# Two attention layers on one core: three tiles instead of two for the values' output, three instead of four for the loads of v, and statistics placed later

## The chip, the cores and the metric

The kernel runs on one core of a Trainium2 chip, as one launch. The metric is device time in microseconds (us). The kernel before takes 3063.1 us, the median of three runs (3060.73, 3063.10 and 3066.85).

## What is computed

The input x is 4 images of 256 channels and 64 by 64 pixels, in float32. Two layers follow each other, each of the form x + layer(gn(x)), where gn is a group norm over 32 groups of 8 channels. Cut to what matters:

```
# layer 0, 8 heads of 32 channels: keys and values come from 2x2 patches, so 1024 of them per image
q = conv1x1(gn(x)); k = conv2x2_stride2(gn(x)); v = conv2x2_stride2(gn(x))
x = x + softmax(scale * q.(k + pos)) . v
# layer 1: each image is cut into 4 areas of 1024 pixels, which attend to themselves
q, k, v = conv1x1(gn(x))
out = softmax(scale * q.k) . v
x = x + conv1x1(out + depthwise_conv7x7(v))
```

Both group norms need the mean and the variance of a whole image before the first of its pixels can be normalized.

## The kernel before, in words

**Blocks, units, steps, phases.** The eight blocks of work are layer 0 for images 0 to 3 (A0 to A3), then layer 1 for images 0 to 3 (B0 to B3). A block is 16 units: 8 chunks of 512 pixels times 2 groups of 4 heads. A unit has 8 steps, one for each 128 keys. The main loop (L1159) takes one and a half steps at a time and calls that a phase, so that three steps are two phases. In a phase TensorE computes the scores of the next step and a half (`s`, L428), then does a piece of side work if one is due (a projection, a slice of the convolution, a row of softmax divisors), then multiplies the exponentials of the phase before with v (`av`, L494). ScalarE makes the exponentials (`p`, L469 and L480); VectorE adds them up to the softmax divisors (`acc`, L504). The scores fill three pairs of PSUM banks in turn, the exponentials six tiles of SBUF (`PB`).

**What sets the order.** Everything beside scores, exponentials and sums is planned ahead by unit and step: `at(unit, step, f)` puts `f` into the main loop at that step, and `task_at` hands a job to a list from which the main loop takes pieces. The order of the instructions on each engine is therefore written by the planner and kept; engines meet through semaphores. All loads and stores but those of the softmax divisors stand in one queue, that of SyncE (SP). An instruction whose wait is not yet over holds up all that stands behind it on its engine or queue. Tiles of one tag share a fixed number of buffers (`bufs`); a tile that takes a used buffer waits for the last reader of what lay there.

**What the change touches.**
- `plan_a` (L551) prepares and runs layer 0 for one image. Ahead of the image's own block it loads each of the 8 chunks of x once for statistics (`look`, L560, tile `xs`), and some steps later, the `lag` of L627, `add_stats` (L563) runs two `bn_stats` on the chunk, one for each half of the channels. `plan_norm` (L335, called at L629) joins the statistics to a shift and a scale. The tiles `xs` share the 6 buffers of the tag `chunk` (L104) with the other chunk tiles: `xa` and `hq` (x to be normalized for keys and values, and for queries), `xc` (residual), `hv` (below), `xm` and `cv` (layer 1).
- `plan_values` (L948) makes v of layer 1 for one chunk: it loads the chunk of layer 0's result (`hv`, L955), ScalarE normalizes it (L957, through L392), TensorE projects it, ScalarE writes the projection to a tile `vout` whose margins VectorE has zeroed (L963, L964, L975), and SP stores `vout` in two layouts: `vala`, for attention (L980), and `vals`, for the convolution (L988). `vout` has 2 buffers.
- `plan_b` (L705) runs layer 1 for one image. For each area it reads v back from `vala` in four loads (`load_v`, L740, tile `vc`, 4 buffers), and VectorE transposes each (`make_v`, L744, L749) into the tile that `av` reads.

Both `vout` and `vc` take 2304 bytes of each partition and buffer.

Of the kernel before, what the change touches and what calls it, by code (L numbers as in the profile page):

```python
# [9 lines left out]
FP = mybir.dt.float32  # L10
# [5 lines left out]
P = 128  # L16
# [11 lines left out]
RC = CH // WW  # L28
# [7 lines left out]
TY, TX, NY, XT, NP, TC = 16, 2, 4, WW // 2 + 4, 88, 8  # L36
# [24 lines left out]
def direct_path(  # L61
# [22 lines left out]
    pool = ctx.enter_context(tc.tile_pool(name="work", bufs=1))  # L84
# [93 lines left out]
    def ps_side(name):  # L178
        if now[0] < 0:
            return ps_pair(name)[:, 0, :]  # L180
        return psum.tile([P, CH], FP, tag=banks[1], name=name, bufs=1)
# [4 lines left out]
    def at(g, j, f):  # L186
        g, j = g + int(j // NKT), int(j % NKT)
        plan.setdefault((g, j), []).append(f)
# [127 lines left out]
    def soon(f):  # L316

        if now[0] < 0:
            f()
        else:  # L320
            quick.append(f)
# [13 lines left out]
    def plan_norm(key, g, j):  # L335

        name = f"{key[0]}{key[1]}"
        made = {}

        def aggregate():  # L340
            for tag, cols in (("mv", 2), ("gmean", 1), ("dev", 1), ("gvar", 1)):
                shape = [P, CT, cols] if cols > 1 else [P, CT]
                made[tag] = pool.tile(shape, FP, tag=tag, name=f"{tag}_{name}", bufs=2)
            mv = made["mv"]
            for t in range(CT):
                V.bn_aggr(out=mv[:, t, :], in_=stats[key][:, t].rearrange("p c s -> p (c s)"))

        def means():
            mv, mean, dev = made["mv"], made["gmean"], made["dev"]
            ps = ps_side(f"gm_{name}")[:, :CT]  # L350
            T.matmul(ps, lhsT=gmat, rhs=mv[:, :, 0], start=True, stop=True)
            S.copy(mean, ps)
            V.tensor_sub(dev, mv[:, :, 0], mean)
            V.tensor_mul(dev, dev, dev)
            V.tensor_add(dev, dev, mv[:, :, 1])

        def variances():
            ps = ps_side(f"gv_{name}")[:, :CT]
            T.matmul(ps, lhsT=gmat, rhs=made["dev"], start=True, stop=True)
            S.activation(made["gvar"], ps, AF.Identity, bias=eps)  # L360
            norm = pool.tile([P, 2, CT], FP, tag="norm", name=f"norm_{name}", bufs=8)
            shift, rstd = norm[:, 0, :], norm[:, 1, :]
            G.tensor_tensor(rstd, made["gvar"], neghalf, ALU.pow)
            if key == ("A", 0):
                V.scalar_tensor_tensor(shift, made["gmean"], -1.0, rstd, ALU.mult, ALU.mult)
            else:
                G.tensor_tensor(shift, made["gmean"], rstd, ALU.mult)
                G.tensor_scalar(shift, shift, -1.0, None, ALU.mult)
            norms[key] = shift, rstd
            known[key] = phase[0] if now[0] >= 0 else -4  # L370

        def quietly(f, n):
            f()
            if key == ("A", 0):
                keep_busy(n)

        if key == ("A", 0):
            at(g - 1, 0, lambda: keep_busy(44))
        at(g, j, aggregate)
        at(g, j + (2 if g >= 0 else 1), lambda: soon(lambda: quietly(means, 4)))  # L380
        at(g, j + (6 if g >= 0 else 3), lambda: soon(lambda: quietly(variances, 10)))
# [169 lines left out]
    def plan_a(b, u, prep):  # L551

        key = ("A", b)

        early = prep - (5 if b == 1 else 8 if b else 0)
# [68 lines left out]
        for c in range(NCH):  # L624
            at(early + c // 2, 4 * (c % 2), lambda c=c: look(c))
            for t in range(CT):
                lag = (5 + 2 * t if b == 1 else 8 + 2 * t if b else 3)  # L627
                at(early + c // 2, 4 * (c % 2) + lag, lambda c=c, t=t: add_stats(c, t))
        plan_norm(key, early + (5 if b > 1 else 4), 3 if b > 1 else 4 if b else 1)  # L629
        for a in range(NAREA):  # L630
            g = prep + (1 + 3.6 * a if b == 1 else 0.05 + 3.7 * a if b else 6 + 2.2 * a)
            at(0, int(NKT * (g - 2.4)), lambda a=a: load(a))
# [48 lines left out]
        for c in range(NCH):  # L681
            g = u + 2 * c
# [22 lines left out]
    def plan_b(b, u):  # L705
        key = ("B", b)
# [11 lines left out]
        kvs, vcs = {}, {}  # L718
# [19 lines left out]
                ks["B", b, a] = k  # L738

        def load_v(a, n):  # L740
            vcs[a, n] = pool.tile([P, 2, 4 * TX, XT], FP, tag="vc", name=f"vc_{b}_{a}_{n}", bufs=4)
            nc.sync.dma_start(vcs[a, n], vala[b][a][:, :, 2 * n : 2 * n + 2].rearrange("t c h f x -> (t c) h f x"))

        def make_v(a, n):  # L744

            if n == 0:
                kvs["v"] = v_tile(("B", b, a))
            v, vc = kvs["v"], vcs.pop((a, n))
            V.transpose(  # L749
                out=v[:, :, 2 * n * HD : 2 * (n + 1) * HD].rearrange("p j (h x) -> p h j x", h=2),  # L750
                in_=vc[:, :, :, 1 : 1 + WW // TX],
            )
            if n == 3:
                vs["B", b, a] = v
# [18 lines left out]
        for a in range(NAREA):  # L773
            g = u + 4 * a
            at(g - 6, 3, lambda a=a: load(a))
            for t in range(CT):
                at(g - 5, 2 + 3 * t, lambda a=a, t=t: later(("hs", b, a), lambda: norm(a, t), after(key, since[a] + 6), True))
            for n in range(4):
                task_at(
                    NKT * (g - 4) + 1 + 4 * n, 2, make_k, a, n // 2, n % 2, due=g - 0.4, ready=normed("hs", b, a)  # L780
                )
            for n in range(4):
                at(g - 4, 3 + 2 * n, lambda a=a, n=n: load_v(a, n))
                at(g - 2, 1 + 2 * n, lambda a=a, n=n: make_v(a, n))
        for c in range(NCH):
            for qd in range(2):
                task_at(
# [76 lines left out]
        for c in range(NCH):  # L864
            g, j = (u + 2 * c + 4, 1) if b < B - 1 or c < NCH - 2 else (u + 2 * c + 3, 7)
# [82 lines left out]
    def plan_values(b, c, start):  # L948

        made = {}  # L950

        def load():
            made["at"] = phase[0]
            made["h"] = chunk_tile(f"hv_{b}_{c}")
            nc.sync.dma_start(made["h"], xmid[b][c])  # L955

        def norm(t):  # L957
            normalize(("B", b), made["h"][:, t, :], made["h"][:, t, :], t)

        def values(t):  # L960
            vout = pool.tile([P, RC, TX, XT], FP, tag="vout", name=f"vout_{b}_{c}_{t}", bufs=2)
            written.append(phase[0])
            V.memset(vout[:, :, :, 0], 0.0)  # L963
            V.memset(vout[:, :, :, 1 + WW // TX :], 0.0)  # L964
            settle(("hv", b, c))
            h = made["h"]
            ps = ps_side(f"vals_ps_{b}_{c}_{t}")
            for tt in range(CT):
                product(
                    ps, lhsT=wqkv_sb[:, tt, 2, t * P : (t + 1) * P], rhs=h[:, tt, :],  # L970
                    start=(tt == 0), stop=(tt == CT - 1),
                )
                if tt == 0:
                    yield
            S.activation(  # L975
                vout[:, :, :, 1 : 1 + WW // TX], ps.rearrange("p (r x f) -> p r f x", r=RC, f=TX), AF.Identity,
                bias=bqkv_sb[:, 2, t : t + 1],
            )
            for n in range(2):
                nc.sync.dma_start(  # L980
                    vala[b][c // 2][2 * (c % 2) + n, :, 4 * t : 4 * t + 4].rearrange("c h f x -> h c (f x)"),
                    vout[:, 4 * n : 4 * n + 4].rearrange("p r f x -> p (r f x)"),
                )

            out = vout.rearrange("p r f x -> p r (f x)")
            for f in range(TX):
                at_row = (1 - f) * (XT - 1)
                nc.sync.dma_start(  # L988
                    vals[b][HALO + c * RC : HALO + (c + 1) * RC, f, t * P : (t + 1) * P, :].rearrange("r p x -> p r x"),
                    out[:, :, at_row : at_row + XT],  # L990
                )
            if t == CT - 1:
                stored[b, c] = True

        when = int(start * NKT)
        at(0, when - 5, load)
        for t in range(CT):
            at(0, when + 5 + t, lambda t=t: later(("hv", b, c), lambda: norm(t), after(("B", b), made["at"] + 6), True))
        for t in range(CT):
            task_at(  # L1000
                when + 7, 2, values, t, due=start + 4,
                ready=lambda: written[-2] + 4 <= phase[0] and normed("hv", b, c)(), lag=1 + 4 * t,
            )
# [153 lines left out]
    f = step = 0  # L1157
    before, credit = [], 0.0
    while f < PHASES or before or plan or side or quick or norms_left or to_add or to_divide:  # L1159
# [16 lines left out]
        _, rate = pressure()  # L1176
# [10 lines left out]
        elif due and not begun():  # L1187
            done_den = 1
            copies[0] += 1
            g = to_divide.popleft()  # L1190
# [644 lines left out]
```

## Time and profile before

| what | value |
|---|---|
| the profiled execution, its own time | 3063.53 us |
| its span, from the first to the last instruction | 3061.5 us |
| median of the three timed runs | 3063.1 us |
| granted clock of TensorE over the span | 0.998 |
| TensorE (PE) busy | 3032.8 us, 99% |
| VectorE (DVE) busy | 2526.2 us, 83% |
| ScalarE (ACT) busy | 2455.9 us, 80% |
| GpSimd (POOL) busy | 433.8 us, 14% |
| share of TensorE in the chain that ended last | 91% |

A page of the profile shows one execution. Busy time counts instructions of an engine, without those that issue DMAs. The timeline lists start and duration, the engine, the line of the kernel, the operation, and out<-in by tile names without their numbers; instructions of one kind that stand together are merged (x3). What stands in brackets is how long the engine stood idle just before, and what ended that. In rows of SP's queue (SPq) the duration is that of issuing, not of moving the data. The chain that ended last follows the last instruction back, at each step to what released it.

### The profile page before, as it was taken

Reading aid. Unit: us, or ns where it says so; the run is one execution under the profiler, and the core shown is the slowest. Engines: PE = TensorE matmul, PEld = TensorE weight load, DVE = VectorE, ACT = ScalarE, POOL = GpSimd, SP = SyncE. Lnnn points to the kernel's source line nnn. Section 1 sums busy time; section 2 is a strip of 40 time slices with the busy share of each in tenths; the row PEclk is TensorE's granted clock in tenths of the full one; section 3 lists DMA queues with packets and bytes.
Section 4 is the critical chain, followed back from the end, with each engine's and each line's share of the span. In section 5 each row is a group of like instructions: output and inputs, shape, how many; then the busy total and the mean of one; then the engine's idle time right before and its main releaser. Section 6 shows DMA issues by size and latency. Waiting matters only on the chain.

```text
span 3061.5 us, 108320 instructions
## 1 busy us (share of the span) xinstructions
PE 3032.8 (99%) x47254; PEld 1280.0 (42%) x47254; DVE 2526.2 (83%) x2769; ACT 2455.9 (80%) x2988; POOL 433.8 (14%) x794
## 2 busy tenths in 40 slices
PE   9999999999999999999999999999999999999998
PEld 6444434444344444333444444444434444443332
DVE  3788988889887787878888888788878888888888
ACT  3888888888887888888888877788777787878885
POOL 0011111111111111111111111111111111111111
PEclk9999999999999999999999999999999999999999
DMA  5244533466354557777866677667755565553232
GB/s 191 51 101 98 126 92 73 109 142 165 83 140 133 143 152 175 189 161 194 204 175 162 156 176 185 152 171 178 176 127 145 144 159 143 149 139 79 50 71 62
DMA packets 644250, 422.73 MB, mean 138 GB/s; under 512 B 409740, under 2 KB 552572, under 8 KB 643768
## 3 DMA queue, kind: packets, MB, share of 16 engines
q1 hardware_dynamic: 619384, 380.11, 49.3%
q0 software_dynamic: 24384, 35.62, 5.1%
q8 instruction: 373, 6.11, 0.9%
q14 instruction: 109, 0.89, 0.1%
HBM read 317.28 MB, written 97.05 MB: 135 GB/s over the span
## 4 chain that ended last, share of the span: by engine, by line
PE 91%; DMA 3%; DVE 2%; ACT 2%; issue 2%; SPq 1%; POOL 0%; DVEq 0%; ACTq 0%; POOLq 0%
PE s L428 31%; PE av L494 26%; PE k0ps L167 4%; PE den L513 4%; PE v0ps L167 4%; PE q1ps L167 4%; PE k1ps L167 4%; PE conv_ps L1048 4%; PE q0ps L167 4%; PE ops L167 4%; PE vals_ps L167 3%; DVE acc L504 1%; ACT p L469 1%; DMA vals<-vout 1%; DMA rows<-vals 1%
## 5 line engine op out<-in xcount | busy, mean ns | idle before, releaser
L504 DVE TENSOR_TENSOR acc<-acc,p 128x1024 f32<-128x1024 f32 x1790 | 2117.4, 1220 | 382.7 <-PE av L494 285.7
L469 ACT ACTIVATE p<-s 128x1024 f32<-128x1024 f32 x1194 | 1159.8, 1025 | 419.3 <-PE s L428 407.6
L480 ACT ACTIVATE p<-s 128x1024 f32<-128x1024 f32 x598 | 619.8, 1036 | 1.5 <-DVE acc L504 0.7
L428 PE MATMUL s<-q,k_A 32*64 32x256 f32 (+1 forms) x10928 | 541.1, 494 | 4.1 <-ACT p L469 3.5
L428 PE MATMUL s<-q,k_B 32*64 32x512 f32 (+1 forms) x10912 | 537.1, 494 | 2.8 <-ACT p L469 2.4
L494 PE MATMUL av<-p,v_A 128*32 128x256 f32 (+1 forms) x4784 | 451.4, 486 | 0.0
L494 PE MATMUL av<-p,v_B 128*32 128x512 f32 (+1 forms) x4776 | 449.4, 487 | 0.0
L428 PEld LDWEIGHTS s<-q,k_B 32*64 32x64 f32 x10912 | 266.0, 130 | 325.1 <-PE s L428 60.4
L428 PEld LDWEIGHTS s<-q,k_A 32*64 32x64 f32 x10928 | 263.2, 130 | 329.1 <-PE s L428 58.5
L537 POOL DMA_DIRECT2D rb<-recs x508 | 251.4, 501 | 510.3 <-DMA recs<-few 497.9
L535 POOL DMA_DIRECT2D recs<-few x127 | 71.3, 561 | 1719.9 <-DVE sums L534 1600.3
L494 PEld LDWEIGHTS av<-p,v_B 128*32 128x32 f32 x4776 | 149.2, 110 | 264.5 <-issue 238.3
L494 PEld LDWEIGHTS av<-p,v_A 128*32 128x32 f32 x4784 | 149.5, 110 | 227.5 <-issue 186.0
L469 ACT ACTIVATE acc<-s 128x1024 f32<-128x1024 f32 x172 | 167.0, 1023 | 80.6 <-PE s L428 80.2
L513 PE MATMUL den<-acc,ones 128*32 128x512 f32 x1024 | 138.5, 605 | 0.9 <-DVE xm L831 0.9
L167 PE MATMUL ops<-cv,wp_sb 128*32 128x512 f32 x1024 | 126.6, 605 | 4.7 <-DVE xm L831 3.5
L527 POOL DMA_DIRECT2D few<-den_sb x127 | 90.5, 713 | 271.9 <-ACT den_sb L526 271.3
L167 PE MATMUL vals_ps<-hv,wqkv_sb 128*32 128x512 f32 x1024 | 124.9, 598 | 0.5 <-issue 0.5
L167 PE MATMUL q1ps<-h,wqkv_sb 128*32 128x512 f32 x1024 | 124.9, 599 | 0.0
L167 PE MATMUL k1ps<-h,wqkv_sb 128*32 128x512 f32 x1024 | 123.0, 597 | 1.7 <-ACT cout L1059 0.9
L167 PE MATMUL q0ps<-hq,wq_sb 128*32 128x512 f32 x1024 | 124.0, 597 | 0.1
L167 PE MATMUL k0ps<-taps,wkv 128*32 128x256 f32 x2048 | 123.9, 383 | 0.0
(102 smaller groups left out, 2089.5 us busy)
## 6 DMA issues: line engine op xcount, KB each, us to landing
rows<-vals SPq DMA_DIRECT2D x384, 195.9 KB
rb<-recs POOLq DMA_DIRECT2D x508, 64.0 KB, 3.6
share<-vals SPq DMA_DIRECT2D x128, 195.9 KB
vala<-vout SPq DMA_DIRECT2D x128, 144.0 KB
vals<-vout SPq DMA_DIRECT2D x128, 144.0 KB
vc<-vala SPq DMA_DIRECT2D x64, 288.0 KB
band<-mats SPq DMA_DIRECT2D x96, 176.0 KB
hq<-in_x SPq DMA_DIRECT2D x32, 512.0 KB
```

Source lines behind the costliest of these rows:

```text
L167: T.matmul(out[cols, :], lhsT=lhsT[:, cols], rhs=rhs, start=start, stop=stop)
L428: T.matmul(out[n : n + WIDE], lhsT=unit[2]()[rows, unit[0], j * P + n : j * P + n + WIDE], rhs=unit[1]()[rows, cols], start=True, stop=True,)
L469: S.activation(p, (a, b)[n], AF.Exp, scale=SCALE)
L480: S.activation(p, c.rearrange("p b (l n) -> p b l n", l=2), AF.Exp, scale=SCALE)
L494: T.matmul(out, lhsT=v[:, j, unit[0] * P + HD * h : unit[0] * P + HD * h + HD], rhs=rhs, start=(j == 0 and not u), stop=(j == NKT - 1), sk ...
L504: V.tensor_add(to, to, p)
L513: T.matmul(dens[g][HD * h : HD * h + HD, :], lhsT=ones, rhs=p(h), start=(n == 0), stop=(n == len(sets) - 1),)
L527: G.dma_start(few[:, 0, :], den_sb[0:P:HD, :].rearrange("h (q n) -> h q n", n=CH // HD))
L535: G.dma_start(recs.rearrange("h (q n) -> (h q) n", n=CH // HD), few[:, 1, :])
L537: G.dma_start(rb[HD * h : HD * h + HD, :], recs[h : h + 1, :].to_broadcast([HD, CH]))
L1048: T.matmul(ps[HD * m : HD * m + HD, (2 * k + i) * size : (2 * k + i + 1) * size].rearrange("p (y x) -> p y x", y=NY), lhsT=band[:, half].r ...
```

## The change

Four edits, in three places:

```
--- before
+++ after
@@ plan_a
         for c in range(NCH):
             at(early + c // 2, 4 * (c % 2), lambda c=c: look(c))
             for t in range(CT):
-                lag = (5 + 2 * t if b == 1 else 8 + 2 * t if b else 3)
+                lag = (5 + 2 * t if b == 1 else 11 + 2 * t if b else 3)
                 at(early + c // 2, 4 * (c % 2) + lag, lambda c=c, t=t: add_stats(c, t))
-        plan_norm(key, early + (5 if b > 1 else 4), 3 if b > 1 else 4 if b else 1)
+        plan_norm(key, early + (5 if b > 1 else 4), 4 if b > 1 else 4 if b else 1)
@@ plan_b
         def load_v(a, n):
-            vcs[a, n] = pool.tile([P, 2, 4 * TX, XT], FP, tag="vc", name=f"vc_{b}_{a}_{n}", bufs=4)
+            vcs[a, n] = pool.tile([P, 2, 4 * TX, XT], FP, tag="vc", name=f"vc_{b}_{a}_{n}", bufs=3)
             nc.sync.dma_start(vcs[a, n], vala[b][a][:, :, 2 * n : 2 * n + 2].rearrange("t c h f x -> (t c) h f x"))
@@ plan_b, g is the unit at which area a begins
             for n in range(4):
-                at(g - 4, 3 + 2 * n, lambda a=a, n=n: load_v(a, n))
-                at(g - 2, 1 + 2 * n, lambda a=a, n=n: make_v(a, n))
+                at(g - 4, 7 + 2 * n + 5 * (n == 3), lambda a=a, n=n: load_v(a, n))
+                at(g - 2, 0 + 2 * n + 3 * (n == 3), lambda a=a, n=n: make_v(a, n))
@@ plan_values
         def values(t):
-            vout = pool.tile([P, RC, TX, XT], FP, tag="vout", name=f"vout_{b}_{c}_{t}", bufs=2)
+            vout = pool.tile([P, RC, TX, XT], FP, tag="vout", name=f"vout_{b}_{c}_{t}", bufs=3)
```

The output tile of the values gets a third buffer and the loads of v lose one, so that the memory stays the same. For images 2 and 3 the two `bn_stats` of a chunk stand three steps, two phases, further behind the chunk's load, and the joining of the statistics one step later. The loads of v for an area stand four steps later (the fourth nine steps later), and their transposes one step earlier (the fourth two steps later). No instruction is added or removed.

## The prediction

> **What bounds the kernel now.** I read the page's shares first, then the chain that ended last.
>
> ```profile
> PE 3032.8 (99%) x47254; PEld 1280.0 (42%) x47254; DVE 2526.2 (83%) x2769; ACT 2455.9 (80%) x2988; POOL 433.8 (14%) x794
> ...
> PE 91%; DMA 3%; DVE 2%; ACT 2%; issue 2%; SPq 1%; POOL 0%; DVEq 0%; ACTq 0%; POOLq 0%
> ```
>
> TensorE is busy for 3032.8 of 3061.5 us, so all its idle time is 28.7 us. The change adds and removes no instruction, and the built programs have the same order on TensorE, ScalarE and GpSimd; only places on VectorE and in SP's queue differ. A gain can only come out of those few microseconds, and a loss only through a new wait that reaches TensorE.
>
> So I looked for phases that last too long. From the starts of the score rows in the timeline, phases with equal work last equally long: 4.62 us with a full projection, 4.65 with a slice of the convolution, 3.76 with the divisors (the shortest of each kind). What a phase takes above that is a stall that TensorE felt. For whole-run waits on the values' output I took the view of the tile `vout`:
>
> ```profile
> its engine sat idle before it (us, times) until:
>   DMA vals<-vout: 10.3, 4
> ```
>
> Writers of `vout` waited 10.3 us for its stores, four times, on ScalarE and VectorE together. The timeline around the worst place:
>
> ```profile
> 1383.23 0.81 ACT L392 ACTIVATE hq<-hq,norm_A 128x512 f32<-128x512 f32 x1 [2.04 <-DMA hq<-in_x]
> ...
> 1385.92 2.00 PE L428 MATMUL s<-q,k_A 32*64 32x256 f32 x32 [1.17 <-ACT p L469]
> ...
> 1388.28 0.70 ACT L975 ACTIVATE vout<-vals_ps,bqkv_sb 128x512 f32<-128x512 f32 x1 [1.50 <-DMA vals<-vout]
> 1388.33 0.07 DVE L963 MEMSET vout<- 128x16 f32 x1 [4.70 <-DMA vals<-vout]
> ...
> 1389.03 1.11 PE L1048 MATMUL conv_ps<-rows,band 88*32 88x128 f32 x32 [1.11 <-ACT vout L975]
> 1389.67 1.03 ACT L469 ACTIVATE p<-s 128x1024 f32<-128x1024 f32 x1 [0.69 <-DVE acc L504]
> ```
>
> Two things are to be seen. The store of `vout` holds ScalarE and VectorE, and TensorE feels it through the bank of `conv_ps` and through late sums. And the first two rows give a rate that I use below: when a load (`hq`) kept ScalarE idle for 2.04 us, TensorE idled for 1.17, so about 0.87 us of a wait on ScalarE is covered.
>
> **The third buffer of vout.** What TensorE lost beside these waits: the phase from 1240.81 to 1246.86 took 6.05 instead of 4.65 (1.40); 1385.92 to 1392.24, 6.32 instead of 4.65 (1.67); the next two, with late sums, 5.23 instead of 4.62 (0.61) and 4.57 instead of 3.76 (0.81). Together **4.49 us**. With three buffers the writer at 1388.28 needs the stores that the zeroing at 1368.45 waited for, long over; the one at 1242.90 needs stores issued by 1214.1. So the waits go. The hq wait at 1383.23 (a phase of 5.00 instead of 3.76) stays: it is another tile. Ends: 4.49 if all goes, 1.40 + 1.67 = 3.07 if the late sums have another cause; I take 4.49, since VectorE's 4.70 us stand right before them.
>
> **Statistics later, on VectorE.** The 32 moved `bn_stats` cost the same 0.69 us each. They waited for a load twice: 0.24 us and
>
> ```profile
> 681.47 0.70 DVE L564 BATCH_NORM_STATS2 st_A<-xs 128x6 f32<-128x512 f32 x1 [0.24 <-DMA xs<-in_x]
> ...
> 703.74 0.69 DVE L564 BATCH_NORM_STATS2 st_A<-xs 128x6 f32<-128x512 f32 x1 [3.04 <-DMA xs<-in_x]
> ```
>
> The phases after it are 0.16 and 0.23 us too long, so the gain is at most **0.39 us**, at least nothing; I take 0.39.
>
> **Statistics later, in SP's queue.** Here the change adds a wait. A load of `xs` takes the buffer of an earlier chunk, and by the built program it waits in SP's in-order queue for that chunk's second `bn_stats`. In both programs the load of chunk 3 of image 3 (677.68 below) waits for the second statistic of chunk 2, which before starts at 676.97 and ends at 677.65.
>
> ```profile
> 676.97 0.68 DVE L564 BATCH_NORM_STATS2 st_A<-xs 128x6 f32<-128x512 f32 x1
> ...
> 682.08 3.60 DVE L504 TENSOR_TENSOR acc<-acc,p 128x1024 f32<-128x1024 f32 x3
> ```
>
> ```profile
> 677.68 0.37 SPq L108 DMA_DIRECT2D xs<-in_x  x1
> ...
> 688.02 0.47 SPq L108 DMA_DIRECT2D xs<-in_x  x1
> ...
> 691.22 0.52 SPq L679 DMA_DIRECT2D xmid<-xc  x1
> 691.80 2.90 SPq L928 DMA_DIRECT2D made<-bands  x2
> 695.43 0.33 SPq L955 DMA_DIRECT2D hv<-xmid  x1
> ```
>
> ```profile
> 699.96 0.86 ACT L392 ACTIVATE hv<-hv,norm_B 128x512 f32<-128x512 f32 x1
> ```
>
> In the new order that statistic stands behind the three sums of 682.08, which end at 685.68, so it ends at 686.4, 8.7 us later. Everything behind the load in the queue moves: ten issues, the load of chunk 4 (688.02), six more issues, and then the load of `hv` (695.43), which ScalarE normalizes at 699.96. In before `hv` had 4.5 us to land. Now chunk 4's load follows its own statistic (behind VectorE's row that ends at 695.0, so 695.7) or the queue (686.4 + 10.3 = 696.7); `hv` follows 7.4 us behind, at 703.1 to 704.1. If VectorE is ahead by the statistic and the 0.24 us that no longer stand in front (0.9), and a gap or two in the queue closes, it is 701. I take 703.1. From issue to landing: 3.8 us where the statistic at 681.47 waited for the load of 677.68; at most 4.5 for `hv` itself; I take 4.0, in between. ScalarE, whose order is fixed, would then idle until 707.1, 7.1 us, and TensorE 0.87 less, **6.3 us**. Ends: 701 + 3.8 gives 3.9 for TensorE, 704.1 + 4.5 gives 7.7. Queued behind `hv` on ScalarE are the exponentials of 700.68, for which the next scores wait. That is the one place: the other loads that are pushed back (for instance `hq` of the first image, 287.0 to 293.5, read at 309.1; the residual of 319.0 to 327, read at 348.4) keep 8 us or more from issue to reader, and the statistics behind late loads are themselves two phases later.
>
> The row that starts at 677.68, 0.03 us behind the statistic, shows a load held in the queue. The Trainium skill says the same (DMA: Bandwidth & Descriptors, section Anatomy of one DMA): a semaphore wait sits on the issuing sequencer, ahead of dispatch; this rule speaks against standing statistics later. Its fit, 2.0 us and bytes by 436 per ns, gives an estimate of 3.2 us for these 512 KB; with it the loss would be 5.5 instead of 6.3 us.
>
> **Loads of v later.** 64 transposes of 0.70 us stay. Placing each new load between its neighbours in SP's queue and adding that load's own time to landing in the trace, all 64 land ahead of their transpose, three by little (1.2, 4.2 and 4.3 us), the rest by 7 or more. The fourth transpose of an area comes 4 to 6 us later; the first `av` on that tile follows at least 20 us after. The fourth load now waits in the queue for the first transpose: 8.1 us at 2358.3 and 4.9 at 2546.7, hardly elsewhere; behind it stand loads read 40 us later. I take nothing. Above nothing: the 4.70 us of idle VectorE above cost TensorE 1.42, so ten waits of 5 us would cost 15; nearest row: no transpose waits in before. Below nothing: the loads of `cv` come a little earlier, and two sums at 2083 and 2325 waited 0.6 and 0.5, so a gain below 0.5.
>
> **Sum.** -4.49 - 0.39 + 6.3 + 0 = +1.4 us, from 3063.53 to 3064.9 for such an execution. The median of before is 0.4 lower, so **3064.5 us**. About 0.2% (6.1 us) is what a measurement of this kernel can tell from no change: I forecast no change, a gain eaten by a new wait.
>
> **Rivals.**
> - *The new wait is covered* (0.25): SP catches up in the idle 14 us before 686, `hv` lands by 701. For it: the queue is emptier then. Against: six issues in a row between chunk 4's load and `hv`, two held by landings. It gives 3063.1 - 4.9 = 3058.2.
> - *The load of hv lands late* (0.18): the hq load read at 1383.23 was issued at 1374.67, 8.6 us to land; issued at 704.1, `hv` would land at 712.7, ScalarE idles 12.7, TensorE 11.9: +7.0, **3070.1**, slower. It decides from a landing at 712 upward. Against: the queue around 695 landed in 3.8 to 6.2 us.
> - *Transposes wait* (0.08): some ten loads of v land late by 3 us; at 1.42 for 4.70 that is 9 us: 3067 without the hv wait, 3073.5 with it.
> - *The third buffer does not help*, since another wait stood behind the store (0.04): 3069.
>
> **How the numbers follow.** The forecast has 0.45. Its own spread (3.9 to 7.7, 4.49 or 3.07, runs 6 us apart) is 3059 to 3069. The range takes in the covered wait, with the runs' spread below it, and the late landing: 3056.5 to 3070.1. Faster by over 0.2% means below 3057.0: 0.10 from the covered wait, 0.05 from the forecast. Slower means above 3069.2: 0.11 from the late landing, 0.06 from transposes, 0.02 from the buffer, 0.06 from the forecast: 0.25. Within: 0.60.
>
> **What would show it.** Right: no wait of `vout` rows on its stores; near 1240 and 1386 phases of 4.65; ScalarE's row of `hv` near 707 with some 7 us idle behind a DMA, and the scores after it idle for 6. Wrong: that row without a wait, idle time ahead of transposes, or a stall in a place where I counted 8 us of slack.

## The result, and the profile after

The changed kernel takes 3069.3 us (median of 20 runs, 3062.6 to 3072.2); the kernel before, on the same chip, 3065.0 (20 runs, 3059.1 to 3069.8). The ratio is **1.0014, 95% interval 1.0008 to 1.0021**: 4.3 us slower, between 2.5 and 6.4. The forecast was 1.4 us slower, which the prediction called no change, since it put what can be told at 0.2%; with 20 runs each the interval leaves 1 out, so this is a small loss. The sign and the main loss were right. Two terms were off, and one loss was in none of the terms.

The profiled execution of the changed kernel took 3070.6 us (span 3068.8). First the page, engines and chain, to set beside the lines of before:

```profile
PE 3032.3 (99%) x47254; PEld 1276.9 (42%) x47254; DVE 2527.2 (82%) x2769; ACT 2455.2 (80%) x2988; POOL 433.9 (14%) x794
...
PE 89%; DVE 3%; DMA 3%; issue 2%; ACT 2%; SPq 1%; POOL 0%; DVEq 0%; ACTq 0%; POOLq 0%
```

Nothing is busier. TensorE's 3032.3 us are those of before, its idle time went from 28.7 to 36.5 us: what changed is waits alone.

**The waits on vout are gone**, as forecast. The view of the tile `vout` has no line for its stores any more:

```profile
its engine sat idle before it (us, times) until:
  PE vals_ps L167: 1.2, 2
```

The timeline of the changed kernel, where before ScalarE and VectorE had stood still for 1.50 and 4.70 us:

```profile
1385.94 0.81 ACT L392 ACTIVATE hq<-hq,norm_A 128x512 f32<-128x512 f32 x1 [1.84 <-DMA hq<-in_x]
...
1388.62 2.00 PE L428 MATMUL s<-q,k_A 32*64 32x256 f32 x32 [0.97 <-ACT p L469]
1389.37 0.71 ACT L975 ACTIVATE vout<-vals_ps,bqkv_sb 128x512 f32<-128x512 f32 x1
```

The writer of `vout` at 1389.37 waits for nothing; the wait for `hq` ahead of it stayed.

**The new wait at hv came**, in the place and at the time that were forecast. In this execution the phases here start 2.1 us earlier than in before (697.2 against 699.3), so take 2.1 from the forecast's times. The timeline, VectorE's statistics, SP's queue, ScalarE and TensorE together:

```profile
674.81 0.67 DVE L564 BATCH_NORM_STATS2 st_A<-xs 128x6 f32<-128x512 f32 x1
...
682.52 0.69 DVE L564 BATCH_NORM_STATS2 st_A<-xs 128x6 f32<-128x512 f32 x1
...
683.23 0.37 SPq L108 DMA_DIRECT2D xs<-in_x  x1
...
692.09 0.68 DVE L564 BATCH_NORM_STATS2 st_A<-xs 128x6 f32<-128x512 f32 x1
...
693.85 0.53 SPq L108 DMA_DIRECT2D xs<-in_x  x1
...
700.96 0.33 SPq L955 DMA_DIRECT2D hv<-xmid  x1
...
704.25 0.81 ACT L392 ACTIVATE hv<-hv,norm_B 128x512 f32<-128x512 f32 x1 [6.30 <-DMA hv<-xmid]
...
706.94 2.90 PE L428 MATMUL s<-q,k_A 32*64 32x256 f32 x32 [5.08 <-ACT p L469]
...
709.76 2.58 PE L167 MATMUL vals_ps<-hv,wqkv_sb 128*32 128x512 f32 x16
```

Read it downwards. The second statistic of chunk 2 ends at 683.21, and 0.02 us later SP issues the load of chunk 3 that was held. Behind it the queue works off what has gathered until 693.75; chunk 3's second statistic has ended by then (692.77), and chunk 4's load goes out at 693.85. Six issues further stands `hv`, at 700.96. It lands, ScalarE starts after 6.30 us of idling, and the scores wait 5.08. The two phases from 697.2 and 706.9 took 9.77 and 6.62 us instead of 4.62: **7.15 us lost**.

**A second stall was not forecast.** The timeline of the changed kernel 780 us later:

```profile
1470.02 0.40 SPq L108 DMA_DIRECT2D hq<-in_x  x1
...
1474.24 1.55 PE L428 MATMUL s<-q,k_A 32*64 32x256 f32 x32
...
1479.87 0.81 ACT L392 ACTIVATE hq<-hq,norm_A 128x512 f32<-128x512 f32 x1 [5.19 <-DMA hq<-in_x]
...
1482.55 2.90 PE L428 MATMUL s<-q,k_A 32*64 32x256 f32 x32 [3.56 <-ACT p L469]
```

The load of `hq` for chunk 7 of image 3 took 9.85 us from issue to its reader. The two phases from 1474.2 lost 3.66 and 1.61 us. The timeline of before has the same load, with 8.46 us to its reader and no wait:

```profile
1465.91 0.39 SPq L108 DMA_DIRECT2D hq<-in_x  x1
...
1474.37 0.92 ACT L392 ACTIVATE hq<-hq,norm_A 128x512 f32<-128x512 f32 x1
```

The table below has what TensorE lost by place: the sum of what phases took above the shortest phase with equal work, as in the prediction. A place is the same phases in every profile, and the heads of the columns give its times in before, in us. The table has all twelve profiles; the experiments are told in the next section.

| kernel | vout buffers, hq loads | 699 to 713 | 1202 to 1402 | 1402 to 1501 | 1800 to 1904 |
|---|---|---|---|---|---|
| before | 2, late | 0.16 | 10.30 | 1.01 | 0.15 |
| before once more (f2) | 2, late | 0 | 8.61 | 1.01 | 1.56 |
| loads of v alone (f3) | 2, late | 0 | 5.70 | 1.01 | 1.73 |
| statistics alone (e2) | 2, late | 7.97 | 9.18 | 1.02 | 2.60 |
| hq moved alone (g1) | 2, moved | 0 | 11.83 | 1.02 | 2.83 |
| after | 3, late | 7.15 | 5.80 | 6.25 | 2.31 |
| after once more (f1) | 3, late | 6.26 | 3.46 | 2.98 | 1.73 |
| chunk 2 put back (g2) | 3, late | 6.91 | 4.25 | 3.84 | 1.66 |
| statistics put back (e1) | 3, late | 0 | 4.95 | 1.33 | 2.87 |
| chunks 2 and 3 put back (e3) | 3, late | 0 | 4.84 | 1.83 | 1.73 |
| e1 and hq moved (e4) | 3, moved | 0 | 3.95 | 1.14 | 1.84 |
| e3 and hq moved (f4) | 3, moved | 0 | 4.19 | 1.01 | 2.03 |

### The profile page after: what moved, and what is told of

The parts are those of the page before. It is cut to its first block, busy times and chain, and to the rows that moved or that the text cites. A ratio compares the mean times of both kernels' runs of the same rounds, so it can differ in the third digit from the quotient of the medians.

```text
span 3068.8 us, 108297 instructions
## 1 busy us (share of the span) xinstructions
PE 3032.3 (99%) x47254; PEld 1276.9 (42%) x47254; DVE 2527.2 (82%) x2769; ACT 2455.2 (80%) x2988; POOL 433.9 (14%) x794
## 4 chain that ended last, share of the span: by engine, by line
PE 89%; DVE 3%; DMA 3%; issue 2%; ACT 2%; SPq 1%; POOL 0%; DVEq 0%; ACTq 0%; POOLq 0%
PE s L428 30%; PE av L494 26%; PE k0ps L167 4%; PE den L513 4%; PE conv_ps L1048 4%; PE q1ps L167 4%; PE k1ps L167 4%; PE q0ps L167 4%; PE v0ps L167 4%; PE vals_ps L167 3%; PE ops L167 3%; DVE acc L504 2%; ACT p L469 1%; DMA share<-vals 1%; DMA h<-xmid 0%
```

## The experiments

Each compares with runs of the kernel before on its own chip. Differences in us are worked out from the ratio and its interval where nothing else is said. In all of them the order of instructions on TensorE, ScalarE and GpSimd is that of before.

**e1: statistics put back.** The changed kernel, with

```
-                lag = (5 + 2 * t if b == 1 else 11 + 2 * t if b else 3)
+                lag = (5 + 2 * t if b == 1 else 8 + 2 * t if b else 3)
-        plan_norm(key, early + (5 if b > 1 else 4), 4 if b > 1 else 4 if b else 1)
+        plan_norm(key, early + (5 if b > 1 else 4), 3 if b > 1 else 4 if b else 1)
```

> The changed kernel with the statistics put back where they stood before (lag 8, joining at step 3); third buffer of vout and later loads of v stay. Theory A: the stall at the load of hv near 697 us (7.15 us of TensorE in the profile after) comes from the statistics alone, so it goes; the waits on vout stay gone (4.49); and the stall near 1474 us (hq, 5.27 us in the profile after, 0.46 at that place before) is the gain of the third buffer given back: SP's queue is full between 1360 and 1490 us, so TensorE comes earlier and the load of hq doesn't. Then the stall near 1474 is here too, 3 to 6 us, and the time is -4.5 + 4.8 = about the time before (within 2 us), some 7 under the changed kernel. Rival B: the stall near 1474 was chance in that one execution, or came from the statistics: then it is absent, and the time is 4 to 5 us under before. Rival C: the stall near 697 has another cause than the statistics: then it stays, and the time is that of the changed kernel.

Measured: ratio to before **0.9994 (0.9985 to 1.0003)**, 3058.6 against 3060.8 us. The timeline of e1, the load of `hv` and its reader, then the load of `hq` and its reader:

```profile
693.81 0.33 SPq L955 DMA_DIRECT2D hv<-xmid  x1
...
698.04 0.88 ACT L392 ACTIVATE hv<-hv,norm_B 128x512 f32<-128x512 f32 x1
```

```profile
1459.56 0.39 SPq L108 DMA_DIRECT2D hq<-in_x  x1
...
1468.12 0.82 ACT L392 ACTIVATE hq<-hq,norm_A 128x512 f32<-128x512 f32 x1 [1.23 <-DMA hq<-in_x]
```

`hv` goes out on time and nobody waits: rival C falls. The wait for `hq` is here too, but with 1.23 us instead of 5.19: the statistics don't make it, and its size was below what I expected. The time, 1.8 us under before (4.6 under to 0.9 over), lies within A's 2 us, and its interval reaches B's 4 to 5: by itself it doesn't tell how much of the gain is given back.

**e2: statistics alone.** The reverse of that edit, on the kernel before.

> The kernel before with the later statistics alone (lag 11, joining at step 4); two buffers of vout, v loads as before. Theory A: the load of hv near 697 goes out 7 us late, ScalarE idles 6 to 7 us, TensorE loses 6.5 to 7.2 us; the four waits on vout stay (about 10 us of idle writers, 4.5 us of TensorE), and near 1474 us no phase is more than 1 us too long. Time 6 to 7 us over before. Rival B (the stall near 1474 comes from the statistics or by chance): a phase of several us too long near 1474 here as well, time 10 to 12 over before. Rival C: no stall near 697, time as before.

Measured: ratio **1.0025 (1.0014 to 1.0036)**, 7.7 us slower (4.3 to 11.0). The timeline of e2 at three places:

```profile
703.69 0.81 ACT L392 ACTIVATE hv<-hv,norm_B 128x512 f32<-128x512 f32 x1 [6.21 <-DMA hv<-xmid]
```

```profile
1392.07 0.70 ACT L975 ACTIVATE vout<-vals_ps,bqkv_sb 128x512 f32<-128x512 f32 x1 [2.49 <-DMA vals<-vout]
1392.12 0.07 DVE L963 MEMSET vout<- 128x16 f32 x1 [5.09 <-DMA vals<-vout]
```

```profile
1478.18 0.89 ACT L392 ACTIVATE hq<-hq,norm_A 128x512 f32<-128x512 f32 x1
```

The stall at `hv` is whole without the rest of the change (7.97 us of TensorE, somewhat more than I expected), the waits on `vout` are back (three, 8.8 us), and `hq` is not waited for. So the wait for `hq` goes with the third buffer, the wait for `hv` with the statistics.

**e3: 4 of the 32 statistics put back**, those of chunks 2 and 3 of image 3:

```
-                lag = (5 + 2 * t if b == 1 else 11 + 2 * t if b else 3)
+                lag = (5 + 2 * t if b == 1 else 8 + 2 * t if b == 3 and c in (2, 3) else 11 + 2 * t if b else 3)
```

> The changed kernel with 4 of the 32 moved statistics put back: those of chunks 2 and 3 of image 3. By theory A these four alone hold the loads of chunks 3 and 4 in SP's queue, and with them the load of hv: the stall near 697 goes (at most 1 us left) and the time is 6.5 to 7.2 us under the changed kernel, within 1 us of the kernel with all 32 put back. Rival C (all the later statistics load VectorE or the queue, and any of them can hold the load): more than 3 us of the stall stay.

Measured: ratio **0.9994 (0.9985 to 1.0003)**, 3058.7 us, that of e1. The stall at `hv` is gone with these four instructions; the other 28 stand later, and the times show no cost of theirs.

**g2: 2 of the 32 put back**, those of chunk 2 alone (`c == 2` in the line above).

> The changed kernel with 2 of the 32 statistics put back: those of chunk 2 of image 3 alone. Theory A, in detail: the load of chunk 3 then goes out on time (near 675.5 us), but the load of chunk 4 still waits for chunk 3's second statistic, which stands late (ends near 692.8 us), and hv comes 6.4 to 7.4 us behind it, at 699 to 700 instead of 700.9: ScalarE still idles 4.5 to 6 us and TensorE loses 4.5 to 6.5 us near 697. Either of two waits alone holds hv, so putting back one of them gains 0 to 2 us, both 7. Rival H: only the first load that is held matters (the one named in the prediction): the stall goes with chunk 2 alone. Rival I: each wait carries its half: 3 to 4 us of stall stay.

Measured: ratio **1.0019 (1.0010 to 1.0028)**, as slow as the whole change. The timeline of g2:

```profile
675.29 0.37 SPq L108 DMA_DIRECT2D xs<-in_x  x1
...
691.00 0.68 DVE L564 BATCH_NORM_STATS2 st_A<-xs 128x6 f32<-128x512 f32 x1
...
691.71 0.38 SPq L108 DMA_DIRECT2D xs<-in_x  x1
...
700.12 0.33 SPq L955 DMA_DIRECT2D hv<-xmid  x1
...
703.32 0.81 ACT L392 ACTIVATE hv<-hv,norm_B 128x512 f32<-128x512 f32 x1 [5.58 <-DMA hv<-xmid]
```

The first load is on time now (675.29 against 683.23), and it helps nearly nothing: the second is held until chunk 3's statistic ends, at 691.68, and `hv` comes 0.8 us earlier than in the changed kernel. TensorE still loses 6.91 us there, so rivals H and I fall. Two waits stand in a row in one queue, and the second alone is enough; the kernel with the first alone was not run.

**e4: e1 with two loads of hq moved ahead.** For chunks 5 and 7 of image 3 the load stands four steps earlier in SP's queue, ahead of 11 issues of `share`, `conv`, `band` and `rows`; its reader stays.

```
         for c in range(NCH):
             g = u + 2 * c
+            if (b, c) in {(3, 5): 4, (3, 7): 4}:
+                at(g - 3, 4 - {(3, 5): 4, (3, 7): 4}[b, c], lambda c=c: sooner(c))
             at(g - 3, 4, lambda c=c: fetch(c))
```

This is the main part of the edit, cut out of the kernel: `sooner` issues the load, and `fetch` then issues it no second time.

> The kernel with the statistics put back, and two loads of hq moved ahead in SP's queue: those of chunks 5 and 7 of image 3, read near 1386 and 1480 us, ahead of 11 issues of share, conv, band and rows. No other instruction moves. Theory A: place in the queue sets when hq lands; the stalls near 1383 (1.0 to 1.5 us) and 1474 (3 to 6 us) go, and the time is 4.5 to 7 us under the kernel with the statistics put back, so 4 to 7 us under before. Rival D: the DMA engines have no room around 1460 us, and whatever is moved ahead makes another load late: rows, hv or xc then wait by about as much, and the time is that of the kernel with the statistics put back.

Measured: ratio **0.9985 (0.9975 to 0.9994)**, 3055.8 us, 4.6 us under before (1.8 to 7.7) and 2.8 under e1 by the medians (the intervals of the two ratios overlap), less than the 4.5 that I expected at least, as the wait to be taken away was smaller. The timeline of e4:

```profile
1456.21 0.47 SPq L108 DMA_DIRECT2D hq<-in_x  x1
...
1469.36 0.94 ACT L392 ACTIVATE hq<-hq,norm_A 128x512 f32<-128x512 f32 x1
```

The load now has 13 us, and neither reader of `hq` waits. A load of `hv` kept ScalarE idle for 1.30 us at 1453.85, but it was issued at 1446.57, ahead of the moved load, and it was waited for without the move as well (0.57 us in after, 1.94 in g2). TensorE's losses between 1202 and 1501 fall from 6.3 in e1 to 5.1 us. The late loads of rival D are not to be seen.

**g1: the same two loads moved, with two buffers of vout**, on the kernel before: the fourth corner.

> The kernel before (two buffers of vout, everything as it was) with only the two loads of hq (chunks 5 and 7 of image 3) moved ahead of 11 issues in SP's queue: the fourth corner beside before, third buffer alone (about -1.8 us) and third buffer with the moved loads (-4.6). Theory A: the moved loads are worth something only where the third buffer has brought TensorE forward; with two buffers the waits on vout near 1240 and 1386 us stay and set the time, and only the wait of hq near 1380 goes (0.4 to 1.2 us of TensorE): time -0.5 to -1 us against before. Rival G: the moved loads are worth their 2.8 us by themselves: -2.5 to -3 us.

Measured: ratio **0.9999 (0.9989 to 1.0008)**: nothing. The timeline of g1 (its lines stand 6 later):

```profile
1378.95 0.82 ACT L392 ACTIVATE hq<-hq,norm_A 128x512 f32<-128x512 f32 x1
...
1386.13 0.70 ACT L981 ACTIVATE vout<-vals_ps,bqkv_sb 128x512 f32<-128x512 f32 x1 [3.29 <-DMA vals<-vout]
```

The wait for `hq` is gone, and the one on `vout` behind it is 3.29 us (1.50 to 2.49 in the four profiles with two buffers and late loads). By the ratios, the third buffer gives 1.8 us (e1, which has the later loads of v as well), the moved loads 0.3, both together 4.6. The intervals are some 2.8 us to either side: rival G's 2.5 to 3 lie near the edge of this one (3.4 faster to 2.4 slower), and the times alone don't settle it. The rows speak against G: two buffers leave no wait for `hq` near 1470 that a moved load could take away.

**f1: the changed kernel once more.**

> The changed kernel once more, unaltered, to see which of its stalls come back in another execution. Theory A2 (after the kernel with the statistics put back, where the wait for hq near 1468 us was 1.23 us on ScalarE and not 5.19): the stall at hv near 697 belongs to the change and comes back with 7.0 to 7.3 us of TensorE; the wait for hq near 1475 comes back too, since the load goes out only 4.7 to 7.3 us before ScalarE needs it (8.5 in the kernel before), but its size goes with the execution, 1 to 5 us; the time is about 5 us over before. Theory A1: the later statistics make SP late there each time: the wait for hq is again about 5 us.

Measured: ratio **1.0010 (1.0001 to 1.0019)**, 3.1 us slower (0.3 to 5.8), less than the 5 that I expected. The timeline of f1:

```profile
703.04 0.81 ACT L392 ACTIVATE hv<-hv,norm_B 128x512 f32<-128x512 f32 x1 [5.87 <-DMA hv<-xmid]
```

```profile
1464.78 0.40 SPq L108 DMA_DIRECT2D hq<-in_x  x1
...
1473.55 0.82 ACT L392 ACTIVATE hq<-hq,norm_A 128x512 f32<-128x512 f32 x1 [2.90 <-DMA hq<-in_x]
```

The wait for `hv` came back with nearly its size (6.26 us of TensorE, a little under what I expected), the wait for `hq` with about half. Theory A2 holds, and the 5.19 us were the largest of five. What sets the size is not settled: the three profiles with all or nearly all of the later statistics waited 5.19, 2.90 and 2.99 us (g2), the two without the stall at `hv` 1.23 (e1) and 1.74 (e3). A part of that stall in it is not ruled out.

**f2: the kernel before once more**, for its profile.

> The kernel before once more, unaltered, for its profile. In the profiles of the changed kernel and of four experiments one projection phase of TensorE near 1805 us (q of layer 1) had a pause of 1.1 to 1.7 us inside a group of matmuls, without a wait, and lost 1.6 to 2.7 us; the profile of before has none. If it is chance, it is here too, with 1 to 3 us in that phase; if it belongs to what the variants share, it is absent here again. The four waits of writers of vout (8 to 11 us in all) come back, and no wait for hq near 1475.

Measured: 3060.1 us, one run. The writers of `vout` waited 7.8 us, three times and not four, and no row of `hq` near 1470 waited. The pause near 1807 is here too, 0.38 us: it is not the change's.

**f3: loads of v alone**, with `bufs=3` for `vc` and the new places of `load_v` and `make_v`, on the kernel before.

> The kernel before with the loads of v alone changed (three buffers, loads and transposes placed later); two buffers of vout, statistics as before. Forecast of the prediction: nothing, within 0.5 us; ratio 1.000; no transpose idle for its load by more than 1 us, TensorE's phases between 1480 and 2700 us as before. Rival E: the later loads cost where they stand behind a waiting fourth load: some transposes wait, 1 to 3 us in all. Rival F: the queue between 1480 and 2700 is eased by the later loads and the time falls by 1 to 2 us.

Measured: ratio **0.9999 (0.9990 to 1.0008)**. One transpose waited, 0.68 us, and TensorE's phases between 1480 and 2700 lost 6.35 us, as in the two profiles of before (5.58 and 6.45). The rows show nothing, as forecast; the interval of the time (3.1 us faster to 2.4 slower) would not tell rivals E and F apart from it.

**f4: what is worth keeping.** e3 and e4 together: third buffer, later loads of v, 28 of the statistics later, two loads of hq moved.

> What the runs so far leave of the change, with both repairs: third buffer of vout, later loads of v, 28 of the 32 statistics later (those of chunks 2 and 3 of image 3 back), and the loads of hq for chunks 5 and 7 of image 3 ahead of 11 issues. The gains add: no wait at hv near 697, none at hq near 1383 and 1475, waits of statistics under 0.5 us: 4.5 to 6 us under before (the kernel with all statistics put back and the same two loads was 4.6 under), and 0 to 0.5 us under that kernel. Rival: the later statistics of the other chunks cost nothing and gain nothing, the two kernels are equal.

Measured: ratio **0.9982 (0.9973 to 0.9991)**, 3054.6 against 3059.9 us: 5.5 us under before (2.8 to 8.3). By its ratio it is not apart from e4, so the later statistics show no gain of their own.

## Why the prediction was right or wrong

- **Load of hv held in SP's queue: right, in its place and its steps.** Forecast issue 703.1 in before's time; measured 700.96 + 2.1 = 703.1. That they agree to 0.1 is luck. The forecast took the statistic's bound for chunk 4's load, while of the two bounds the queue came last here (693.75 against 692.77 for the statistic); and chunk 2's statistic ended 1.1 us before its forecast (683.21 + 2.1 against 686.4), where the prediction had named 0.9 but not taken it. With the queue free, in g2, the statistic held the load. Landing: 4.0 us forecast, 3.29 measured, and 3.15 to 3.23 in f1, e2 and g2. The fit of the Trainium skill that the prediction used (DMA: Bandwidth & Descriptors, Anatomy of one DMA; the page gives it for the GpSimd path, this load is SP's) makes 3.2 us: for this load page and trace agree.
- **TensorE's share of that wait: mis-sized.** The step "ScalarE would then idle 7.1 us, and TensorE 0.87 less, 6.3 us" had two errors that cancel in part. ScalarE idled 5.6 to 6.3 us (four profiles). TensorE lost not less but more: 7.15, 6.26, 7.97 and 6.91, a mean of 7.07. The rows after the stall show why: besides the idle 5.08 us, the next scores took 2.90 instead of 1.55 and the projection 2.58 instead of 1.92. Together these are 7.09. After ScalarE has started again, TensorE's weight loads wait for it once more, 0.58 us for an exponential (707.85) and 0.78 for the second half of `hv` (709.76). The 0.87 was taken from a wait of 2 us, and for short waits it holds: near 1470, ScalarE's waits for `hq` of 1.23, 1.74, 2.90 and 2.99 us (e1, e3, f1, g2) cost TensorE's two phases 0.33, 0.84, 2.01 and 2.11, so 0.9 of each is covered. Of the 5.19 us in after nothing is covered (5.27). So the step failed by carrying the rate from 2 us to 7; where between 3 and 5 us the cover ends, no run shows.
- **Third buffer, 4.49: the waits went, but the gain didn't stay.** Between 1202 and 1402 us the four profiles with two buffers and late hq loads lost 8.44 on average (5.70 to 10.30), the five with three buffers 4.66 (3.46 to 5.80): a gain of 3.8, inside the 3.07 to 4.49 of the prediction, though the profiles scatter by more than that. Between 1402 and 1501 the same nine lost 1.01 (1.02 at most) and 3.25 (1.33 to 6.25): 2.2 given back, and about 1.5 us left. With the loads moved (e4, f4) the means are 4.07 and 1.08, and 4.3 us are left. The failed step is "Ends: 4.49 if all goes": it took the time saved at 1386 as saved at the end.
- **What I didn't look for.** I went through the loads that the change pushes back, and found 8 us or more between issue and reader. I took that for slack, although I had read a landing of 8.6 us for the `hq` load of 1374.67. I didn't go through loads that stay while their reader comes forward. The load of `hq` for chunk 7 had 8.46 us in before (8.0 to 10.1 in the other three with two buffers and late loads) and needed 8.2 to 9.9: its margin was small at best. It issues no sooner when TensorE is sooner: in all nine profiles where it stands late, SP issues it 0.02 us after the landing of a load of `share` that stands eight issues ahead, as the profile infers it. Counted from one and the same phase near 1230, it goes out after 231.6 us on average with two buffers and 231.3 with three, and ScalarE is free for it after 240.7 and 237.3: the reader came 3.4 us sooner, the load less than 0.4. The rival that another wait stands behind the store was in the list with 0.04 and "the third buffer does not help"; that is what happened to some three fifths of the gain, but at the next late load and not on `vout` itself.
- **Loads of v: 0, right** (f3). **Statistics on VectorE: 0.39**, not to be told from 0: the rows' 3.28 us of waits fell to 0.54, yet f4 and e4 differ by less than their intervals.
- **Balance of the runs:** +7.07 at `hv`, -1.5 net for the third buffer, 0 for the rest, is +5.5 us; the ratios say +4.3 (2.5 to 6.4) and +3.1 (0.3 to 5.8). The forecast's +1.4 was too low mostly by the third buffer, 4.49 against 1.5. The profiled pair differs by 7.3 us in span, more than the medians: its wait for `hq` was the largest of five, and 2.16 us lie in a phase near 1815 that before had lost in its second profile as well (f2).

Argued and not varied by itself: why the load of `hq` takes 8.2 to 9.9 us where `hv`, of the same size, takes 3.2. The bytes ahead in the queue differ. Behind the load of `share` whose landing lets `hq` go stand seven more transfers, 1.4 MB together, and with `hq` itself 2.0 MB; from its issue to its reader the core moved 2.0 to 2.1 MB in each of the five profiles (213 to 245 GB/s). For `hv`, with loads of 22 KB around it, it moved 0.55 to 0.60 MB (172 to 187 GB/s). So each load took about as long as the bytes up to its own end. It was not tried to move `hv` ahead of the held loads of `xs`; by the order in which the buffers are taken, its own would be one for which the same wait stands.

## What to carry to other kernels

Moving work later on a compute engine can delay the loads that reuse its buffers, and with them every load behind in the same queue; look for the first tile behind the held load whose reader has less than its landing time to spare, and put back only the instructions that hold it. When a wait is taken away, list the loads downstream whose reader now comes sooner while their queue is full: the gain ends at the first one without margin, and moving that load up is part of the same edit.

## What the runs showed of the hardware

- Landing time depended on the place and, as argued above, on the bytes ahead: 512 KB of `hv` near 700 us took 3.15 to 3.29 us in four profiles, 512 KB of `hq` near 1470 took 8.2 to 9.9 in five. The mean busy share of the DMA engines was 0.84 in both stretches (690 to 705 and 1460 to 1480 of the changed kernel), so that share doesn't tell the two apart. The fit that agreed for `hv` would have been too short by 5 to 7 us for `hq`.
- TensorE can pause inside a group of matmuls without any wait that the profile shows. From the changed kernel's timeline:

```profile
1816.33 1.05 PE L167 MATMUL q1ps<-h,wqkv_sb 128*32 128x512 f32 x5
...
1818.52 1.48 PE L167 MATMUL q1ps<-h,wqkv_sb 128*32 128x512 f32 x10 [1.13 <-issue]
```

Eleven of the twelve profiles have it behind the same fifth matmul of that phase, 0.38 to 1.67 us long, with 1.4 to 2.7 us lost in that phase; the first profile of before has none there. It belongs to no part of the change. The traces show what it goes with. Queue q8 brings 16 KB blocks that the profile calls instruction, 373 of them, one per 8.2 us in the mean. In the eleven, one such block starts 13.2 to 14.6 us after the one before it, and the pause ends 2.3 to 2.7 us after its start; in the first profile of before the same block starts 9.4 us after the one before it, and there is no pause. The twelve profiles have 19 such pauses of over 0.3 us between 100 and 3000 us, and each ends 2.3 to 2.7 us after a block that started 11 us or more after the last. So a late block of instructions goes with the pause; why the block is late was not tested.
